# A two-layer graph network on one core: the second layer's step reordered, its results taken after the step's last matrix product

## The chip, the cores and the metric

The kernel runs on one core of a Trainium2 chip. The metric is the device time of one execution in microseconds (us). Before the change the median of 10 runs is 3380.35 us (3376.93 to 3386.58). The engines are TensorE (PE; PEld is its weight load), VectorE (DVE), ScalarE (ACT), GpSimd (POOL) and SyncE (SP), which only issues transfers here.

## What is computed

There are 12500 nodes with 32 features and 200000 edges, sorted by their destination. Two layers follow each other, each as x = x + layer(relu(layernorm(x))). The first sums the scaled source rows of each node's edges and multiplies by a 32x32 matrix. The second puts a small network on every edge and takes the mean over each node's edges:

```python
x_j = x[j_idx]; x_i = x[i_idx]
msg = concatenate([x_i, x_j - x_i], axis=-1)
h = relu(msg @ W1 + b1)      # 64 -> 64
h = relu(h @ W2 + b2)        # 64 -> 128
h = relu(h @ W3 + b3)        # 128 -> 64
m = h @ W4 + b4              # 64 -> 32
s = segment_sum(m, i_idx)
out = s / maximum(cnt, 1)
```

`j_idx` is an edge's source, `i_idx` its destination.

## The kernel before

**What comes before the loop in question.** The first layer (lines 598 to 840) also writes two tables to DRAM, `tab_i` and `tab_j`: for each node its part of `msg @ W1 + b1` as a destination and as a source. What the second layer needs per edge is one row of each, and their sum. The change leaves the first layer alone.

**The second layer** (lines 843 to 999) goes over the edges in chunks of 512 (`CHUNK`: 4 tiles of 128 edges, `TPC`), two chunks at a time. Such a pair takes one step of the loop; there are 391 chunks and so 196 pairs (`NPAIR`). The last pair has one chunk with three tiles of edges. The edges are sorted, so a chunk's destinations lie in a window of 128 nodes, which moves on by 32 nodes (`STEP`) a chunk. For pair m the work is:

- `gather_in` (896): eight indirect transfers that GpSimd issues (line 211), each fetching 128 rows of `tab_j` into `gj`. `gj` has 6 buffers.
- `prepare` (877), three steps ahead: SyncE loads the window of `tab_i` into `ai` (5 buffers) and the edges' relative destinations, spread over all partitions, into `row` (4 buffers).
- `turn` (888): VectorE compares `row` with the partition number (892) and so makes the one-hot matrices that pick rows of `ai`.
- `first` (904): TensorE makes a 1x8 product that only waits for the gathers (908), transposes `gj` (912), and adds the rows of `ai` by the one-hots (916), all into one PSUM tile p1. ScalarE applies relu and writes h1 (920).
- `second` (923): VectorE makes the one-hots of destinations `hot` (584). TensorE multiplies h1 by W2 into p2 (930); ScalarE adds the bias, applies relu and writes h2 (932).
- `third` (934): TensorE multiplies h2 by W3 into p3 (940); VectorE takes the maximum with minus the bias and writes h3 (943).
- `fourth` (947): TensorE sums h3 over the edges of each node with `hot` (958). The sums of two pairs, a group, gather in one half of the PSUM tile `both`, one bank whose halves alternate.
- `add_messages` (962), after each group's second pair: the sums are added to or copied into an accumulator in SBUF by VectorE (560) and ScalarE (558). After four groups `finish_nodes` (853) runs: VectorE prepares counts and the residual (858 to 866), TensorE multiplies by W4 (869), VectorE divides and adds (872, 873) and SyncE writes the rows of `out`.

All of it is under a manual schedule: each engine runs its instructions in the order in which the Python code issues them, and the framework adds the semaphore waits that the data need. The order in a step comes from `lags` and `todo` (977 to 997): at step m the stages `first`, `fourth`, `third`, `second` are issued for different pairs, with the first one step after the gather, the second three, the third four and the fourth five (one less for the last five pairs, but not below one). Each stage issues its matrix products and at once what takes them from PSUM. p1 and p3 have two buffers each, p2 has one.

## Time and profile before

| | |
|---|---|
| median of 10 runs | 3380.35 us |
| the profiled execution, its own time | 3381.98 us |
| its span, from the first to the last instruction | 3380.0 us |
| TensorE busy / VectorE / ScalarE / GpSimd, of the span | 74% / 54% / 33% / 74% |
| the second layer's gathers, first start to last end | 1401.3 to 3352.2 us |
| last VectorE instruction | 3374.65 us |

The profile is one execution. Its page gives each engine's busy time, the costliest groups of instructions (by line and operation, with the idle time of the engine ahead of them and what ended it), and the chain that ended last; the trace answers further questions, such as instructions in order of time, or busy times and the granted TensorE clock of a stretch. A granted clock of 1.00 is full speed. Matrix products are pipelined and their ends modelled, so the distance from one group's start to the next one's is a better price than the stated duration. In float32 each product is shown as several passes, so counts of passes are larger than those of products in the code.

### The profile page before, as it was taken

To read this page: it belongs to the slowest core of one execution; us is meant where nothing else is said; L and a number is where in the kernel's file an instruction comes from. 1 tells how busy PE (TensorE), PEld (TensorE's weight loads), DVE (VectorE), ACT (ScalarE), POOL (GpSimd) and SP (SyncE) were. 2 spreads that over 40 slices of the span, in tenths; PEclk is the share of its full clock that TensorE was granted. 3 is DMA by queue.
4 is the path that set the end of the run, shared out by engine and by line. 5 is a ranking of instruction groups with operands and counts; after the bars stand their busy time and mean duration, and the time that the engine had idled before them with its cause. 6 is when DMAs were issued, how large, how long until landed. Compare 5 with 4: busy or idle time off the path is not lost. (4 is left out here: it accounts for less than half of the span.)

```text
span 3380.0 us, 54122 instructions
## 1 busy us (share of the span) xinstructions
PE 2511.4 (74%) x20860; PEld 1782.5 (53%) x20860; DVE 1815.9 (54%) x4113; ACT 1116.0 (33%) x2034; POOL 2502.0 (74%) x2655
## 2 busy tenths in 40 slices
PE   3772788888888888477778676777777777777777
PEld 2660566666666666244545454545454544545545
DVE  7995787788878887233333333333333333333333
ACT  0003676677666775112122221121212111221121
POOL 7777777777777777477777777777777777777775
PEclk9995998999999998588887888787878788777788
DMA  4113112122222222222222222222222222222221
GB/s 97 15 15 79 26 28 34 31 36 35 32 36 33 33 35 44 44 62 59 62 59 61 62 63 59 61 61 59 62 60 62 59 62 59 63 59 62 60 60 30
DMA packets 234664, 170.64 MB, mean 50 GB/s; under 512 B 156040, under 2 KB 182888, under 8 KB 234400
## 3 DMA queue, kind: packets, MB, share of 16 engines
q0 software_dynamic: 84320, 75.96, 14.1%
q1 hardware_dynamic: 131338, 85.26, 9.4%
q10 hardware_dynamic: 18742, 5.89, 0.9%
q8 instruction: 168, 2.75, 0.3%
q14 instruction: 96, 0.79, 0.1%
HBM read 153.98 MB, written 12.92 MB: 49 GB/s over the span
## 5 line engine op out<-in xcount | busy, mean ns | idle before, releaser
L211 POOL DMA_INDIRECT gj<-tab_j,src_j x1563 | 1474.9, 944 | 511.4 <-issue 420.6
L211 POOL DMA_INDIRECT rows<-tab_hn,src_j x816 | 771.2, 945 | 255.4 <-issue 195.0
L791 ACT ACTIVATE count<-count_two 128x858 bf16<-128x858 f32 x491 | 434.7, 885 | 286.8 <-PE count_two L789 260.1
L943 DVE TENSOR_TENSOR h<-p,b3n 128x512 f32<-128x512 f32 x196 | 135.3, 690 | 727.5 <-PE p L940 727.5
L940 PE MATMUL p<-w3s,h 128*128 128x64 f32 x3128 | 444.7, 302 | 0.0
L940 PEld LDWEIGHTS p<-w3s,h 128*128 128x128 f32 x3128 | 416.9, 215 | 47.1 <-issue 38.7
L932 ACT ACTIVATE h<-p,b2s 128x1024 f32<-128x1024 f32 x196 | 217.8, 1111 | 661.0 <-PE p L930 661.0
L908 PE MATMUL p<-gj,ident 128*1 128x8 f32 x392 | 39.1, 174 | 506.1 <-DMA gj<-tab_j,src_j 506.1
L738 PE MATMUL st<-count,table 128*128 128x104 bf16 (+1 forms) x6076 | 376.3, 217 | 48.0 <-ACT count L791 22.1
L738 PEld LDWEIGHTS <-table 128*128 128x128 bf16 x6076 | 348.8, 99 | 89.8 <-issue 29.4
L908 PEld LDWEIGHTS p<-gj,ident 128*1 128x1 f32 x392 | 21.8, 80 | 678.1 <-issue 666.1
L920 ACT ACTIVATE h<-p 128x512 f32<-128x512 f32 x196 | 117.0, 597 | 790.1 <-PE p L916 790.1
L726 DVE TENSOR_TENSOR oh<-keys,kept 128x2574 bf16<-128x2574 f16 x246 | 365.5, 1488 | 12.3 <-PE count_third L789 12.3
L958 PEld LDWEIGHTS ps<-hot,h 128*64 128x64 f32 x3126 | 270.4, 189 | 174.6 <-issue 164.0
L789 PE MATMUL count_two<-oh,lo 128*128 128x429 bf16 x982 | 276.3, 363 | 93.7 <-ACT count L791 83.8
L560 DVE TENSOR_TENSOR acc<-acc,ps 64x64 f32<-64x64 f32 (+1 forms) x198 | 44.7, 226 | 537.4 <-PE ps L958 504.8
L916 PE MATMUL p<-turned,ai 128*64 128x512 f32 x782 | 328.9, 932 | 0.0
L958 PE MATMUL ps<-hot,h 128*64 128x128 f32 x3126 | 295.6, 351 | 0.5 <-DVE h L943 0.5
L211 POOL DMA_INDIRECT rows_early<-tab_h,src_j x224 | 216.4, 966 | 71.7 <-issue 47.2
L892 DVE TENSOR_TENSOR turned<-row,kept 128x512 f32<-128x512 f16 x391 | 249.7, 680 | 24.5 <-PE p L916 21.4
L791 ACT ACTIVATE count<-count_third 128x416 bf16<-128x416 f32 x491 | 252.0, 513 | 0.0
L584 DVE TENSOR_TENSOR hot<-rel_h,kept 128x512 f32<-128x512 f16 x391 | 249.2, 679 | 0.0
(201 smaller groups left out, 3026.2 us busy)
## 6 DMA issues: line engine op xcount, KB each, us to landing
row<-rel_row SPq DMA_DIRECT2D x195, 256.0 KB
gj<-tab_j,src_j POOLq DMA_INDIRECT x1563
rows<-tab_hn,src_j POOLq DMA_INDIRECT x816
ai<-tab_i SPq DMA_DIRECT2D x195, 64.0 KB
srow<-hi_row SPq DMA_DIRECT2D x64, 98.0 KB
rows_early<-tab_h,src_j POOLq DMA_INDIRECT x224
tab_j<-nu_aij SPq DMA_DIRECT2D x23, 128.0 KB
tab_i<-nu_aij SPq DMA_DIRECT2D x23, 128.0 KB
```

Source lines behind the costliest of these rows:

```text
L211: nc.gpsimd.indirect_dma_start(out=tile_ap, out_offset=None, in_=table, in_offset=bass.IndirectOffsetOnAxis(ap=col, axis=0))
L584: nc.vector.tensor_tensor(hot, rel_h[:, g * TPC : (g + 1) * TPC][:, :, None].to_broadcast([P, TPC, W]), lanes_f[:, None, :W].to_broadcast( ...
L726: nc.vector.tensor_tensor(oh, keys[:, :, i : i + 2][:, :, None, :].to_broadcast([P, 3, KW, 2]), count_h[:, None, :, :].to_broadcast([P, 3, ...
L738: nc.tensor.matmul(ps[:, : tiles * WD], table[:, h, :], c[:, :tiles, h, :], start=(h == 0), stop=(h == PART - 1))
L789: nc.tensor.matmul(ps[:, k, :w], lo[:, i % TPC // 2, :, i % 2], oh[:, k0 + k, :w, i % 2], start=True, stop=True)
L791: nc.scalar.activation(counts[g][:, t, a:b, :].rearrange("p (k h) d -> p k (h d)", k=len(ranges)), ps[:, :, :w], AF.Copy)
L892: nc.vector.tensor_tensor(turned, v["row"][:, k], part_f.to_broadcast([P, CHUNK]), op=OP.is_equal)
L916: nc.tensor.matmul(p1[k * HID : (k + 1) * HID].rearrange("p t e -> p (t e)"), v["ai"][:, k], v["turned"][k], start=False, stop=True, skip_ ...
L932: nc.scalar.activation(h2[:, :n], p2[:, :n], AF.Relu, bias=b2s)
L940: nc.tensor.matmul(p3[:, k * TPC + t, :], v["h2"][:, k, t * P : (t + 1) * P], w3s, start=True, stop=True)
L943: nc.vector.tensor_tensor(h3[:, :n], p3[:, :n], b3n[:, None, :].to_broadcast([P, n, HID]), op=OP.max)
L958: nc.tensor.matmul(ps[k * HID : (k + 1) * HID, o : o + W], v["h3"][:, k * TPC + t, :], v["hot"][k][:, t, :], start=(i == 0 and t == 0), st ...
```

## The change

The lags become fixed: first 1, second 2, third 4, fourth 6 steps after the gather (clipped at the end of the loop, where several pairs then fall in one step). In a step TensorE's work is issued first, in the order `fourth`, `third`, `first`, then a pause's work of `finish_nodes`, then `second`. What takes the products from PSUM is split off into `past_first` to `past_fourth` and issued after all of these, `past_second` first. `ends[step]` is the last product of the step's `second`, and an extra dependency (`behind`) makes h3's instruction wait for it, and the gathers and the loads of `ai` for that of an earlier step. `hot` is made after h3 and no longer ahead of the second stage. The PSUM tiles of the stages are allocated once (`firsts`, `thirds`, `whole`) instead of from pools per pair; `hot` has 3 buffers in place of 4, h1 also. `finish_nodes` has one pause more, ahead of the product with W4. `gather` now returns its instruction.

```diff
     def gather(tile_ap, table, col):
-        nc.gpsimd.indirect_dma_start(
+        return nc.gpsimd.indirect_dma_start(
...
+        firsts = [pp1.tile([P, TPC, P], F32, name=f"p1_{k}") for k in range(2)]
+        thirds = [pp2.tile([P, 2 * TPC, HID], F32, name=f"p3_{k}") for k in range(2)]
+        whole = pp2.tile([P, 2, CHUNK], F32, name="p2")
...
             nc.vector.tensor_add(z, z, x1[:, at, :])
+            yield
             po = message[:, :n]
...
+        ends = {}
+
+        def behind(r, step):
+            if step in ends:
+                tc.add_manual_dep(
+                    r.ins, ends[step].ins.name,
+                    mybir.DependencyInfo(mybir.DependencyClass.Sync, mybir.DependencyReason.DATA))
...
-            nc.sync.dma_start(ai[:, :n], bass.AP(
+            r = nc.sync.dma_start(ai[:, :n], bass.AP(
...
+            behind(r, m - AHEAD - 2)
...
-                gather_chunk(gj[:, :, k, :], tab_j[:, :], g)
+                for t in range(min(TPC, NTR - g * TPC)):
+                    c = g * TPC + t
+                    behind(gather(gj[:, t, k, :], tab_j[:, :], src_j[:, c : c + 1]), m - 5)
...
-            h1 = ep.tile([P, CHUNK], F32, name="h1", bufs=4)
-            nc.scalar.activation(h1, p1.rearrange("p t e -> p (t e)"), AF.Relu)
-            v["h1"] = h1
+            v["p1"] = p1
+
+        def past_first(m):
+            v = live[m]
+            h1 = v["h1"] = ep.tile([P, CHUNK], F32, name="h1", bufs=3)
+            nc.scalar.activation(h1, v["p1"].rearrange("p t e -> p (t e)"), AF.Relu)
 
         def second(m):
...
-                nc.tensor.matmul(p2[:, k], w2s[s, :], v["h1"][s, :], start=True, stop=True)
+                ends[step] = nc.tensor.matmul(p2[:, k], w2s[s, :], v["h1"][s, :], start=True, stop=True)
+
+        def past_second(m):
+            v = live[m]
+            n = len(halves(m))
             h2 = v["h2"] = ep.tile([P, 2, CHUNK], F32, name="h2")
-            nc.scalar.activation(h2[:, :n], p2[:, :n], AF.Relu, bias=b2s)
+            nc.scalar.activation(h2[:, :n], v["p2"][:, :n], AF.Relu, bias=b2s)
...
-            h3 = ep.tile([P, 2 * TPC, HID], F32, name="h3")
-            nc.vector.tensor_tensor(
-                h3[:, :n], p3[:, :n], b3n[:, None, :].to_broadcast([P, n, HID]), op=OP.max)
-            v["h3"] = h3
+
+        def past_third(m):
+            v = live[m]
+            n = len(halves(m)) * TPC
+            h3 = v["h3"] = ep.tile([P, 2 * TPC, HID], F32, name="h3")
+            behind(nc.vector.tensor_tensor(
+                h3[:, :n], v["p3"][:, :n], b3n[:, None, :].to_broadcast([P, n, HID]), op=OP.max), step)
+            v["hot"] = [hot_of(ep, 2 * m + k, f"hot{k}", 3) for k in halves(m)]
...
-        def add_messages(k4):
+        def past_fourth(m):
+            k4, i = divmod(m, GRP // 2)
+            if i < GRP // 2 - 1 and m < NPAIR - 1:
+                return
...
+            for stage, lag in ((first, 1), (second, 2), (third, 4), (fourth, 6)):
+                todo[min(m + lag, NPAIR - 1 + (first, second, third, fourth).index(stage) + 1)].append((m, stage))
+        for step, now in enumerate(todo):
...
+            order = [(m, stage) for stage in (fourth, third, first) for m, s in now if s is stage]
+            for m, stage in order:
+                stage(m)
             advance(running)
...
+            seconds = [m for m, s in now if s is second]
+            for m in seconds:
+                second(m)
+            for m in seconds:
+                past_second(m)
+            for stage in (first, third, fourth):
+                for m, s in order:
+                    if s is stage:
+                        past[stage](m)
+            if step + 1 < NPAIR:
+                turn(step + 1)
```

More of the change, by code (lines that the diff above doesn't have):

```diff
@@ L843, in gnn_kernel @@
     with tc.manual_schedule(), tc.tile_pool(name="prep", bufs=3) as prep, tc.tile_pool(name="e1", bufs=3) as ep, tc.tile_pool(name="fn", bufs=2) as fp, tc.tile_pool(
-        name="p1_ps", bufs=2, space=bass.MemoryType.PSUM
+        name="p1_ps", bufs=1, space=bass.MemoryType.PSUM
     ) as pp1, tc.tile_pool(name="p2_ps", bufs=1, space=bass.MemoryType.PSUM) as pp2:
@@ L901, in gather_in @@
                 g = 2 * m + k
-                gather_chunk(gj[:, :, k, :], tab_j[:, :], g)
+                for t in range(min(TPC, NTR - g * TPC)):
+                    c = g * TPC + t
+                    behind(gather(gj[:, t, k, :], tab_j[:, :], src_j[:, c : c + 1]), m - 5)
         def first(m):
             v = live[m]
-            p1 = pp1.tile([P, TPC, P], F32, name="p1")
+            p1 = firsts[m % 2]
             nc.tensor.matmul(
@@ L918, in first @@
                     start=False, stop=True, skip_group_check=True)
-            h1 = ep.tile([P, CHUNK], F32, name="h1", bufs=4)
-            nc.scalar.activation(h1, p1.rearrange("p t e -> p (t e)"), AF.Relu)
-            v["h1"] = h1
+            v["p1"] = p1
[3 more added lines that the diff above has]
+            nc.scalar.activation(h1, v["p1"].rearrange("p t e -> p (t e)"), AF.Relu)
         def second(m):
             v = live[m]
-            v["hot"] = [hot_of(ep, 2 * m + k, f"hot{k}", 4) for k in halves(m)]
-            n = len(halves(m))
-            p2 = pp2.tile([P, 2, CHUNK], F32, name="p2")
+            p2 = v["p2"] = whole
             for k in halves(m):
                 s = slice(k * HID, (k + 1) * HID)
-                nc.tensor.matmul(p2[:, k], w2s[s, :], v["h1"][s, :], start=True, stop=True)
+                ends[step] = nc.tensor.matmul(p2[:, k], w2s[s, :], v["h1"][s, :], start=True, stop=True)
+        def past_second(m):
+            v = live[m]
+            n = len(halves(m))
             h2 = v["h2"] = ep.tile([P, 2, CHUNK], F32, name="h2")
-            nc.scalar.activation(h2[:, :n], p2[:, :n], AF.Relu, bias=b2s)
+            nc.scalar.activation(h2[:, :n], v["p2"][:, :n], AF.Relu, bias=b2s)
         def third(m):
             v = live[m]
-            n = len(halves(m)) * TPC
-            p3 = pp2.tile([P, 2 * TPC, HID], F32, name="p3", bufs=2)
+            p3 = v["p3"] = thirds[m % 2]
             for k in halves(m):
@@ L975, in gnn_kernel @@
         turn(0)
-        def lags(m):
-            less = min(1, max(0, m - (NPAIR - 6)))
-            return [max(1, lag - less) for lag in (1, 3, 4, 5)]
-        stages = (first, second, third, fourth)
+        past = {first: past_first, second: past_second, third: past_third, fourth: past_fourth}
         todo = [[] for _ in range(NPAIR + 6)]
         for m in range(NPAIR):
-            for stage, lag in zip(stages, lags(m)):
-                todo[m + lag].append((m, stage))
-        for m, now in enumerate(todo):
-            if m < NPAIR:
-                gather_in(m)
-            if m + AHEAD + 1 < NPAIR:
-                prepare(m + AHEAD + 1)
-            advance(running)
-            for k, stage in now:
-                stage(k)
-                if stage is fourth and (k % (GRP // 2) == GRP // 2 - 1 or k == NPAIR - 1):
-                    add_messages(k // (GRP // 2))
-            if m + 1 < NPAIR:
-                turn(m + 1)
+            for stage, lag in ((first, 1), (second, 2), (third, 4), (fourth, 6)):
+                todo[min(m + lag, NPAIR - 1 + (first, second, third, fourth).index(stage) + 1)].append((m, stage))
+        for step, now in enumerate(todo):
+            if step < NPAIR:
+                gather_in(step)
+            if step + AHEAD + 1 < NPAIR:
+                prepare(step + AHEAD + 1)
+            order = [(m, stage) for stage in (fourth, third, first) for m, s in now if s is stage]
+            for m, stage in order:
+                stage(m)
+            advance(running)
+            seconds = [m for m, s in now if s is second]
[9 more added lines that the diff above has]
+                turn(step + 1)
         while running:
```

## The prediction

> **What bounds the kernel now.** I read the page's costliest groups first, for the second layer's loop (the lines from 908 on). Columns: busy, mean ns of one | idle before, what ended it.

> ```profile
> L211 POOL DMA_INDIRECT gj<-tab_j,src_j x1563 | 1474.9, 944 | 511.4 <-issue 420.6
> L908 PE MATMUL p<-gj,ident 128*1 128x8 f32 x392 | 39.1, 174 | 506.1 <-DMA gj<-tab_j,src_j 506.1
> ```

> The gathers fill GpSimd. Of the 511.4 us idle, 35.35 stands ahead of the very first gather (timeline, 1401.29 us: it waits for the first layer's last table rows). The rest is (1474.9 + 511.4 - 35.35)/1563 = 1.248 us a gather, 0.944 of work and 0.30 of issue, with no longer gap. A step has eight: 9.98 us. TensorE's first matmul of a step, L908, waits for a gather to land. So GpSimd sets 1401 to 3352 us, and TensorE follows.

> Next the busy time by stretches: the loop, then three stretches around its end. Columns: length, busy time (instructions) of PE, PEld, DVE, ACT, POOL, granted TensorE clock, DMA share, GB/s.

> ```profile
> 1401.00:3350.00 1949.00, 1445.29 (x9060) 952.08 (x9060) 676.52 (x1330) 384.51 (x618) 1472.98 (x1561) 0.80 0.27 60
> 3340.00:3351.00 11.00, 9.04 (x70) 6.60 (x72) 4.32 (x13) 2.12 (x4) 8.48 (x9) 0.84 0.14 28
> 3351.00:3365.00 14.00, 14.00 (x63) 9.21 (x65) 2.38 (x5) 1.90 (x3) 0.94 (x1) 0.52 0.06 11
> 3365.00:3380.00 15.00, 7.76 (x67) 6.06 (x64) 4.48 (x14) 1.09 (x2) 0.00 (x0) 0.84 0.04 9
> ```

> In the loop TensorE works 1445/195 = 7.41 us a step and has about 2.5 spare. After the last gather (3352.2) GpSimd is idle and TensorE with its followers sets the end: the **drain**, from 3350.17, when pair 194's first stage starts, to 3374.65, when the last VectorE instruction ends.

> Last the timeline, for the price of each stage. First a step at full clock, then rows of the drain:

> ```profile
> 1502.53 0.20 PE L908 MATMUL p<-gj,ident 128*1 128x8 f32 x2 [1.78 <-DMA gj<-tab_j,src_j]
> 1502.66 0.65 PE L912 MATMUL p<-ident,gj 128*128 128x128 f32 x4
> 1503.24 1.08 PE L916 MATMUL p<-turned,ai 128*64 128x512 f32 x4
> 1504.15 1.04 PE L958 MATMUL ps<-hot,h 128*64 128x128 f32 x16
> 1505.13 2.00 PE L940 MATMUL p<-w3s,h 128*128 128x64 f32 x16
> 1507.05 1.13 PE L930 MATMUL p<-h,w2s 64*128 64x512 f32 x4
> ...
> 3354.10 1.98 PE L958 MATMUL ps<-hot,h 128*64 128x128 f32 x16
> 3356.01 3.68 PE L940 MATMUL p<-w3s,h 128*128 128x64 f32 x16
> 3359.61 2.08 PE L930 MATMUL p<-h,w2s 64*128 64x512 f32 x4
> ...
> 3371.44 0.87 PE L958 MATMUL ps<-hot,h 128*64 128x128 f32 x6 [0.52 <-DVE h L943]
> ```

> From start to start, at full clock: first stage 1.62, fourth 0.98, third 1.92, second 1.13, together 5.65. At half clock: fourth 1.85 (1495.54 to 1497.39), third 3.60, second 2.08, first 2.94 (1492.60 to 1495.54), together 10.47.

> **The change part by part.** Call E the end of a step's second stage, now TensorE's last work in every step that has one.

> *Gathers, index loads.* Count and order on GpSimd and SyncE stay the same, and the first gather keeps its waits. Gather m now waits for E of step m-5 in place of the first stage in that step: four steps, 40 us, old. The ai load waits for E of the step before and is needed three to four steps later; the row load queued behind it on SyncE is needed two steps later, some 20 us. All of it costs nothing under that cover. Without cover, each late us of TensorE would be one of the whole loop.

> *A new wait on TensorE.* VectorE's and ScalarE's work on a step's products now starts after E: 0.11 us (the observed gap from L930's end to L932), then L943 0.61 and two L584 1.19 start to start, then the accumulator: add, copy, add, copy (L560, L558), 2515.60 to 2516.68, 1.08. The next fourth stage starts a step with the matmuls into the one bank that these copies read, so every second step, after a group's end, TensorE waits 0.11 + 0.61 + 1.19 + 1.08 + 0.06 = **3.05 us**. Before, the sums were taken in the middle of a step, under the third stage. Queued behind it are that step's third, first and second stages, and on them ScalarE's and VectorE's next round. Per two steps TensorE needs 2 x 7.41 + 3.05 = 17.9 us, GpSimd 19.97. GpSimd hides it, with 2.1 us to spare. So **the loop gains and loses nothing**: TensorE's idle 2.5 us is not the bound, and no instruction leaves GpSimd.

> *Lags.* The fourth stage runs 6 steps after the gather and not 5, the third 4, so more work is left when the gathers end. Full clock, from 3350.17:
> - Step 195, first and second: 1.62 + 1.13. E = 3352.92.
> - Step 196: wait 3.05, fourth 0.98, third 1.92, half a first (last pair, one chunk: 0.13 + 0.58 + 0.46), second 1.13. E = 3361.17.
> - Step 197: fourth 0.98, third 1.92, half a second 0.56. E = 3364.63.
> - Step 198: the wait, with the longer sums of a node group's end (3345.49 to 3347.32, 1.83 instead of 1.08): 3.80; fourth 0.98, third 1.92: 3371.33. Half a third follows under VectorE's work.
> - Step 199: the last fourth needs VectorE's L943 and two L584 of pair 194, then L943 and L584 of pair 195: 0.11 + 0.61 + 1.19 + 0.42 + 0.68, and 0.04 to start: 3374.38, and 0.87: 3375.25.
> - VectorE: four sums 1.39 (two took 0.67 at 3372.35), one result 0.60, five small operations 1.05, the other result 0.55: end 3378.84.

> That is **4.2 us** later than 3374.65. All at half clock (the same sum with 2.94, 1.85, 3.60, 2.08, the waits unchanged) it ends near 3393.4: **18.75 us** later. Which clock? The stretch 3351 to 3365 shows TensorE without a pause and still 0.52 granted, so in a drain with two waits of 3 to 4 us and a third in step 199 about half of the work should run at half clock, as in before's own drain: (4.2 + 18.75)/2 = **11.5 us**.

> [...]

> *Fixed PSUM tiles, smaller hot and h1 rings, one more pause in the node finish.* Two p1, two p3 and one p2 tile were there before; the readers of a step end about 3 us after E, and the same tile is written again later than that. Nothing either way in the loop (cover: GpSimd's 2.1 us); in the drain they are in the sum.

> **Sum.** 3381.98 for the profiled execution (span 3380.0 and 2.0 around it) + 0 in the loop + 11.5 in the drain = 3393.5. It lies 1.6 above the median of the runs shown, 3380.35, so on the median's scale 3391.9; I say **3392 us**, 0.34% slower. A measurement of this kernel can tell about 0.2%, 6.8 us.

> **Rivals.**
> 1. *Not slower: the drain runs at nearly full clock.* Place: steps 195 to 199. Price +4.2 us, 3384.5. It decides while less than (6.8 - 4.2)/(18.75 - 4.2) = 18% of the drain's work is at half clock. For it: 0.84 granted on both sides of the slow stretch. Against it: 0.52 within, and the waits that the change adds there. 13%.
> 2. *TensorE becomes the bound.* The 3.05 us wait itself lowers the clock, and third and fourth now come first after it. Two steps then cost 3.05 + 11.3 + 9.64 x the share of work at half clock; past 58% this exceeds 19.97. At 65% it is 20.6, 0.33 us a step, over 195 steps +64: 3456 with the drain. At 100% 24.0, +395. For it: single steps of 10 to 12 us (1841.95: 11.98). Against it: 0.80 granted over the loop, and that TensorE, when late, has no idle time left to lower it. 8%.
> 3. *Faster.* The drain alone can't do it: at full clock and with the waits of steps 196 and 198 gone it is 4.2 - 3.05 - 3.80 = -2.65 us, within 0.2%. It would take cheaper gathers: 0.01 us off the 0.30 of issue is 1563 x 0.01 = 16 us, 3376 with the drain. Nothing on GpSimd changes, so 3%.
> 4. *The waits don't do what they say*, being met at once by other work: then only the lags are left, -2.65 at full clock and some +5 with half of the work slow: 3378 to 3385. 4%.

> **How the numbers follow.** The forecast, a late drain with an unchanged loop, has 72%, 3387 to 3399. Rival 2 is slower too: 8%. Rivals 1 and 4 lie within 0.2%: 17%. Rival 3: 3%. So slower 0.80, same 0.17, faster 0.03. The range, 3381 to 3408, leaves out rival 2's far part, rival 3 and a little of rival 4; its upper part holds the half-clock drain, 3380.35 + 18.75 = 3399, and a TensorE just past its limit (0.05 us a step).

> **What would show it.** In the changed kernel's profile: the gather group still 1.248 us each, the last starting near 3351.3; a wait of L984 on ScalarE's L558, some 3 us, about 95 times; from the last gather's landing to VectorE's end about 36 us where it was 24.5. It is wrong if gathers show gaps that end on PE (rival 2), if L984 doesn't wait, or if the end comes as early as before.

## The result, and the profile after

The changed kernel takes **3393.64 us** (median of 8 runs, 3390.16 to 3394.79) against 3380.85 (28 runs of the kernel before on the same chip): ratio **1.0037**, 95% interval 1.0028 to 1.0045. That is 12.8 us slower.

One correction to what stands ahead of the prediction. In the code of before a step begins with its oldest pair: fourth, third, second, first. The order given there is the same cycle, begun at the wait. So before already went oldest first, and what the change moves on TensorE is the first stage, from behind the second to ahead of it.

The costliest groups of the changed kernel, that answer to those shown of before (busy, mean ns of one | idle time before, what ended it):

```profile
L211 POOL DMA_INDIRECT gj<-tab_j,src_j x1563 | 1475.0, 944 | 511.5 <-issue 448.7
L984 PE MATMUL ps<-hot,h 128*64 128x128 f32 x3126 | 277.5, 334 | 288.1 <-ACT acc L558 275.8
```

The gathers are where they were: the same 944 ns, 511.5 us of idle time against 511.4. What is new is the second line, 288 us of idle time. Before, the same products were L958 and had 0.5:

```profile
L958 PE MATMUL ps<-hot,h 128*64 128x128 f32 x3126 | 295.6, 351 | 0.5 <-DVE h L943 0.5
```

The waits of the changed kernel in the loop, 1401 to 3350 us, show where it was taken from (us in total, times, longest):

```profile
PE ps L984 <- ACT acc L558: 272.9, 91, 3.1
PE p L926 <- DMA gj<-tab_j,src_j: 116.5, 64, 16.0
```

Before, TensorE waited in the loop almost for the gathers alone, at L908 (L926 now):

```profile
PE p L908 <- DMA gj<-tab_j,src_j: 504.3, 177, 16.0
```

273 us of that are now a wait for the sums, 3.0 us each time, and most of the rest went into a slower clock. The loop and the drain by stretches (length, busy time of PE, PEld, DVE, ACT, POOL, granted clock, DMA share, GB/s):

```profile
1401.00:3350.00 1949.00, 1557.71 (x9022) 994.14 (x9022) 666.49 (x1310) 361.46 (x614) 1471.46 (x1560) 0.75 0.27 60
...
3351.02:3384.94 33.92, 27.02 (x170) 21.56 (x170) 12.95 (x37) 3.58 (x8) 0.00 (x1) 0.70 0.03 5
```

In the loop the clock fell from 0.80 to 0.75, and TensorE's work rose from 1445 to 1558 us. It cost nothing, since GpSimd sets the pace. The second line is the drain, from the end of the last gather to the end of VectorE's last instruction: 33.92 us, where before had 22.43 (3352.22 to 3374.65). The timeline of TensorE shows what it is made of:

```profile
3346.80 0.20 PE L926 MATMUL p<-gj,ident 128*1 128x8 f32 x2
...
3348.52 1.13 PE L949 MATMUL p<-h,w2s 64*128 64x512 f32 x4
3352.62 1.09 PE L984 MATMUL ps<-hot,h 128*64 128x128 f32 x16 [2.97 <-ACT acc L558]
3353.65 3.20 PE L962 MATMUL p<-w3s,h 128*128 128x64 f32 x16
...
3364.42 1.12 PE L949 MATMUL p<-h,w2s 64*128 64x512 f32 x2
3369.26 1.98 PE L984 MATMUL ps<-hot,h 128*64 128x128 f32 x16 [3.71 <-DVE acc L560]
3371.16 5.38 PE L962 MATMUL p<-w3s,h 128*128 128x64 f32 x24
3376.47 4.96 PE L984 MATMUL ps<-hot,h 128*64 128x128 f32 x38
```

The two waits for the sums, 2.97 and 3.71 us, are no longer hidden by gathers. Around the end of each the clock falls to half for a while: it is 0.50 from 3354.20 to 3361.03 and from 3367.85 to 3381.51 us (16 passes of L962 take 3.20 us, where 2.00 is full clock; 24 take 5.38, where 2.89 is). At the end three fourth stages stand in a row.

One execution's first layer may end some us earlier or later than another's (the first gather starts at 1401.29 us before, at 1397.84 in the changed kernel), so the traces are best compared from the first gather on. In the loop column of this table stands the time from the first gather's start to the last one's end, in the drain column the time from there to the end of VectorE's last instruction, and beside it the clock granted in the drain. The kernels are explained below; "us against before" is the difference of loop plus drain.

| kernel | ratio of medians (95%) | loop | drain | clock in the drain | us against before |
|---|---|---|---|---|---|
| before | 1 | 1950.9 | 22.4 | 0.71 | 0 |
| changed | 1.0037 (1.0028 to 1.0045) | 1953.2 | 33.9 | 0.70 | +13.7 |
| changed, sums early | 1.0012 (1.0003 to 1.0021) | 1951.4 | 25.8 | 0.89 | +3.9 |
| changed, spare products | 1.0016 (1.0007 to 1.0025) | 1952.1 | 26.7 | 0.98 | +5.4 |
| changed, last pairs forward | 1.0069 (1.0056 to 1.0082) | 1955.5 | 39.3 | 0.61 | +21.4 |
| changed, sums early, last pairs forward | 1.0032 (1.0021 to 1.0044) | 1955.3 | 29.5 | 0.70 | +11.5 |
| before, longer lags | 1.0017 (1.0008 to 1.0026) | 1950.8 | 26.7 | 0.68 | +4.2 |
| before, spare products | 0.9989 (0.9980 to 0.9998) | 1950.7 | 16.6 | 1.00 | -6.1 |
| before, short lags | 0.9982 (0.9973 to 0.9992) | 1952.4 | 15.1 | 0.95 | -5.8 |
| before, short lags and spare products | 0.9995 (0.9986 to 1.0004) | 1952.3 | 16.0 | 0.98 | -5.1 |

### The profile page after: what moved, and what is told of

The parts are those of the page before. It is cut to its first block, busy times and chain, and to the rows that moved or that the text cites. A ratio compares the mean times of both kernels' runs of the same rounds, so it can differ in the third digit from the quotient of the medians.

```text
span 3390.2 us, 54031 instructions
## 1 busy us (share of the span) xinstructions
PE 2629.4 (78%) x20860; PEld 1830.9 (54%) x20860; DVE 1813.4 (53%) x4113; ACT 1094.4 (32%) x2034; POOL 2502.0 (74%) x2655
## 4 chain that ended last, share of the span: by engine, by line
POOL 34%; issue 14%; DMA 7%; PE 5%; DVE 2%; ACT 0%; SPq 0%; POOLq 0%; ACTq 0%; DVEq 0%
POOL gj L211 34%; DMA gj<-tab_j,src_j 6%; PE p L962 1%; PE p L949 1%; PE p L934 1%; PE ps L984 1%; PE p L930 0%; DVE hot L584 0%; PE nu_ps L512 0%; PE nu_ps L473 0%; PE st L738 0%; DVE acc L560 0%; DVE h L969 0%; DVE oh L726 0%; DMA rows<-tab_hn,src_j 0%
## 5 line engine op out<-in xcount | busy, mean ns | idle before, releaser
L211 POOL DMA_INDIRECT gj<-tab_j,src_j x1563 | 1475.0, 944 | 511.5 <-issue 448.7
L211 POOL DMA_INDIRECT rows<-tab_hn,src_j x816 | 770.7, 945 | 254.0 <-issue 193.5
L962 PE MATMUL p<-w3s,h 128*128 128x64 f32 x3128 | 545.6, 347 | 0.0
L962 PEld LDWEIGHTS p<-w3s,h 128*128 128x128 f32 x3128 | 514.0, 257 | 46.9 <-issue 46.9
L984 PE MATMUL ps<-hot,h 128*64 128x128 f32 x3126 | 277.5, 334 | 288.1 <-ACT acc L558 275.8
L984 PEld LDWEIGHTS ps<-hot,h 128*64 128x64 f32 x3126 | 218.3, 168 | 484.3 <-ACT acc L558 361.1
L934 PE MATMUL p<-turned,ai 128*64 128x512 f32 x782 | 308.0, 876 | 0.0
L949 PE MATMUL p<-h,w2s 64*128 64x512 f32 x782 | 284.0, 809 | 0.0
L211 POOL DMA_INDIRECT rows_early<-tab_h,src_j x224 | 216.6, 967 | 71.8 <-issue 48.8
L908 DVE TENSOR_TENSOR turned<-row,kept 128x512 f32<-128x512 f16 x391 | 250.4, 682 | 28.6 <-PE p L934 22.6
L584 DVE TENSOR_TENSOR hot<-rel_h,kept 128x512 f32<-128x512 f16 x391 | 249.3, 679 | 0.0
L789 PEld LDWEIGHTS <-lo 128*128 128x128 bf16 x1473 | 131.5, 100 | 178.5 <-issue 119.3
L949 PEld LDWEIGHTS p<-h,w2s 64*128 64x128 f32 x782 | 78.5, 246 | 225.4 <-issue 224.3
L342 PE MATMUL deg_ps<-hi,lo 128*128 128x98 bf16 x1563 | 159.3, 271 | 44.4 <-DVE lo L325 44.4
```

What stands on the lines that cost most here:

```text
L211: return nc.gpsimd.indirect_dma_start(out=tile_ap, out_offset=None, in_=table, in_offset=bass.IndirectOffsetOnAxis(ap=col, axis=0))
L584: nc.vector.tensor_tensor(hot, rel_h[:, g * TPC : (g + 1) * TPC][:, :, None].to_broadcast([P, TPC, W]), lanes_f[:, None, :W].to_broadcast( ...
L789: nc.tensor.matmul(ps[:, k, :w], lo[:, i % TPC // 2, :, i % 2], oh[:, k0 + k, :w, i % 2], start=True, stop=True)
L908: nc.vector.tensor_tensor(turned, v["row"][:, k], part_f.to_broadcast([P, CHUNK]), op=OP.is_equal)
L934: nc.tensor.matmul(p1[k * HID : (k + 1) * HID].rearrange("p t e -> p (t e)"), v["ai"][:, k], v["turned"][k], start=False, stop=True, skip_ ...
L949: ends[step] = nc.tensor.matmul(p2[:, k], w2s[s, :], v["h1"][s, :], start=True, stop=True)
```

## The experiments

**The sums at once.** Theory: what the drain lost is mostly the wait for the sums. Rival: it is the lags.

```diff
             for m, stage in order:
                 stage(m)
+                if stage is fourth:
+                    past_fourth(m)
...
-            for stage in (first, third, fourth):
+            for stage in (first, third):
```

> The changed kernel with one part undone: a group's sums (past_fourth) are issued right after the fourth stage's products again, so they run under the third stage; order, lags and all other late readers stay. My theory, that all of the loss sits in the drain after the last gather and that the loop hides TensorE's wait: the waits of L984 on L558 go (3.05 us every second step), the gathers stay at 1.248 us each, and only the drain gains, 3.05 + 3.80 us of waits and 1 to 3 us of clock: 3384 to 3388, against 3393.6 of the changed kernel. Rival, that the waits in the loop cost time as well: more than 12 us below the changed kernel, at or under the kernel before. Rival, that only the longer lags cost: no gain, 3392 to 3395.

Measured: 3383.9 us (11 runs), ratio 1.0012 (1.0003 to 1.0021), at the lower end of what the theory expected. TensorE's idle time is back at the gathers, as the page shows:

```profile
L926 PE MATMUL p<-gj,ident 128*1 128x8 f32 x392 | 39.1, 175 | 509.8 <-DMA gj<-tab_j,src_j 509.7
```

So of the 12.8 us some 8.5 (1.0037 - 1.0012, times 3380) go with taking the sums late. Not all of that is waiting: the drain's clock rose too, from 0.70 to 0.89. The rest stays with lags, order and the other late readers.

**Longer lags alone.** The kernel before, its order and its readers unchanged, with the lags of the change:

```diff
-        def lags(m):
...
-            for stage, lag in zip(stages, lags(m)):
-                todo[m + lag].append((m, stage))
+            for i, (stage, lag) in enumerate(zip(stages, (1, 2, 4, 6))):
+                todo[min(m + lag, NPAIR + i)].append((m, stage))
```

> The kernel before with only the change's lags, 1, 2, 4 and 6, clipped at the end as in the change, once more for the same reason; order and readers as before. Theory (longer lags leave one third stage and two fourth stages more behind the last gather): 1.92 + 2 x 0.98 = 3.9 us at full clock, 3.60 + 2 x 1.85 = 7.3 at half; ratio to before 1.0010 to 1.0023. Rival (the lags cost nothing, all of the loss is the late sums and the clock they bring): 0.9994 to 1.0006.

Measured: 3385.55 us (11 runs), before beside it 3378.25; ratio 1.0017 (1.0008 to 1.0026), in the middle of what was expected. Loop as before, drain 26.7 against 22.4 us. Together with the run above this splits the loss as it was measured, each part with the clock that came with it: the lags are worth 4 to 6 us, the late sums 8 to 10, which is a little more than the 12.8 to be shared out. A split at one clock follows below.

**The clock in the drain of the changed kernel.** Four spare products in each of the two waits of the drain keep TensorE streaming and take nothing away:

```diff
+            if step in (NPAIR, NPAIR + 2):
+                v = live[NPAIR - 1]
+                for _ in range(4):
+                    nc.tensor.matmul(
+                        firsts[1][:HID].rearrange("p t e -> p (t e)"), v["ai"][:, 0], v["turned"][0], start=True, stop=True)
             for m, stage in order:
                 stage(m)
```

> The changed kernel with spare products in the waits of steps 196 and 198, once more, for the same reason. Theory (the clock that these waits bring makes most of the drain's loss): 5 to 9 us faster than the changed kernel, ratio to before 1.0012 to 1.0024. Rival (the readers behind E set the end, the clock is worth little): 1.0032 to 1.0044.

Measured: 3386.99 us (11 runs), ratio 1.0016 (1.0007 to 1.0025), as the theory expected; in the traces the drain is 7.2 us shorter than that of the changed kernel. The timeline around the second wait (L1021 are the spare products):

```profile
3365.01 3.65 PE L1021 MATMUL p<-turned,ai 128*64 128x512 f32 x8
3368.79 1.09 PE L984 MATMUL ps<-hot,h 128*64 128x128 f32 x16
3369.82 2.89 PE L962 MATMUL p<-w3s,h 128*128 128x64 f32 x24
3372.64 2.95 PE L984 MATMUL ps<-hot,h 128*64 128x128 f32 x38
```

The fourth stage starts as late as without them, 4.83 us behind the start of the second (4.84 without), for it still waits for the sums. What comes behind runs at full clock, 0.98 over the drain: 24 passes of L962 in 2.89 us and not 5.38, 38 of L984 in 2.95 and not 4.96.

**The clock in the drain of before.** The same question on the other side: three spare products ahead of L908, in TensorE's wait for the gathers, for pairs 191 to 194.

```diff
             p1 = pp1.tile([P, TPC, P], F32, name="p1")
+            if NPAIR - 5 <= m < NPAIR - 1:
+                for _ in range(3):
+                    nc.tensor.matmul(
+                        p1[:HID].rearrange("p t e -> p (t e)"), v["ai"][:, 0], v["turned"][0], start=True, stop=True)
```

> The same kernel as the one with spare products before L908 for pairs 191 to 194, once more, since before itself took 4304 us in that call, with TensorE short of instructions. Theory (before's own drain is slow because the clock stays at half from 3351.3 to 3364.9): 4 to 6.5 us faster than before, ratio 0.9981 to 0.9989. Rival (the drain is set by GpSimd's last gathers and by the readers): 0.9997 to 1.0003, or 1.0005 to 1.0010 by the spare products' own time.

Measured: 3375.92 us (11 runs), before beside it 3380.78; ratio 0.9989 (0.9980 to 0.9998), as the theory expected. The drain of before, and that of this kernel, by the same columns as above:

```profile
3352.22:3374.65 22.43, 20.54 (x124) 15.19 (x122) 6.86 (x19) 2.99 (x4) 0.00 (x0) 0.71 0.03 6
```

```profile
3346.56:3363.12 16.56, 14.67 (x124) 11.04 (x122) 6.87 (x19) 3.00 (x4) 0.01 (x1) 1.00 0.05 8
```

The same 124 passes of TensorE, the same VectorE and ScalarE work: 14.67 us of TensorE instead of 20.54. Half clock was 5.9 us of before's own drain. This matters for the account: at full clock on both sides, changed against before is loop plus drain 1978.8 against 1967.3, and 3386.99 against 3375.92 us in the medians, taken side by side. **The change costs 11 us at an equal clock.** Half clock costs either drain 6 to 8 us and adds only some 2 us to the difference.

One more trace splits these 11 us at full clock. A second execution of before with the longer lags (from the set of runs described further down, where the loop was slower) had a drain at 1.00. From the start of pair 194's first stage to the end of VectorE's last instruction, by the same columns: before with spare products, before with the longer lags, the changed kernel with spare products.

```profile
3344.94:3363.12 18.18, 16.29 (x133) 11.74 (x132) 6.87 (x19) 3.00 (x4) 1.32 (x2) 1.00 0.06 11
4288.76:4311.19 22.43, 19.89 (x182) 15.35 (x180) 10.78 (x32) 4.52 (x7) 0.67 (x1) 1.00 0.04 8
3349.07:3379.10 30.03, 28.35 (x200) 17.81 (x200) 14.28 (x39) 4.84 (x9) 2.69 (x3) 0.98 0.04 8
```

The longer lags alone cost 4.25 us, the order and the late readers 7.6 more (11.9 together from this start), of which the two waits for the sums are 6.7 (2.97 and 3.71 in the changed kernel).

**Fewer steps behind the last gather, two misses.** In the changed kernel the last pairs were pulled forward: third lag 3 and fourth lag 4 for the last five, fourth lag 5 for the three ahead of them.

```diff
-            for stage, lag in ((first, 1), (second, 2), (third, 4), (fourth, 6)):
+            late = m - (NPAIR - 8)
+            for stage, lag in ((first, 1), (second, 2), (third, 3 if late >= 3 else 4), (fourth, 4 if late >= 3 else 5 if late >= 0 else 6)):
```

> The changed kernel with the lags of the last eight pairs shortened in the last steps with gathers (third 3 and fourth 4 for the last five pairs, fourth 5 for the three ahead), so that two fourth stages and one third stage fewer are left for the drain, as in the kernel before. Late sums and order stay. Theory: the drain loses 2 x 0.98 + 1.92 = 3.9 us of products at full clock, 7.3 at half: 3386 to 3391. Rival, that only the late waits cost: 3392 to 3395.

Measured: 3402.16 us (6 runs), ratio 1.0069 (1.0056 to 1.0082): slower than the changed kernel, against the expectation. Its timeline:

```profile
3349.71 3.63 PE L984 MATMUL ps<-hot,h 128*64 128x128 f32 x32 [4.76 <-ACT acc L558]
...
3361.78 1.97 PE L984 MATMUL ps<-hot,h 128*64 128x128 f32 x16 [3.72 <-DVE acc L560]
...
3372.85 0.43 PE L984 MATMUL ps<-hot,h 128*64 128x128 f32 x2 [1.39 <-DVE hot L584]
```

The expectation took it that TensorE has time left in the last steps for the work that is pulled forward. It hasn't: the first stage of pair 194 starts 1955.9 us after the first gather, in the changed kernel 1949.0. And where a fourth stage comes only one step behind its third, it waits for the one-hots (L584) too, which this order makes only after the second stage. With the sums at once added to these lags the same was expected to be as fast as before, within 0.1%:

> Both at once: sums issued right after the fourth stage and the shorter lags at the end, the rest of the change (order, fixed tiles, late readers of the other stages, late dependencies of gathers and loads) kept. Theory: the two parts of the drain add up to the whole loss, so 3379 to 3384, the kernel before within 0.1%. Rival, that something else of the change costs too (a cost in the loop, or the late readers themselves): 3386 or more.

Measured: 3390.68 us (6 runs), ratio 1.0032 (1.0021 to 1.0044), a miss as well. The waits for the sums are gone, those for the one-hots stand in nearly every step of the drain:

```profile
3344.39 2.13 PE L984 MATMUL ps<-hot,h 128*64 128x128 f32 x18 [1.48 <-DVE hot L584]
...
3353.96 1.59 PE L984 MATMUL ps<-hot,h 128*64 128x128 f32 x16 [1.48 <-DVE hot L584]
```

So long lags and late readers belong together: with the readers behind the last product, a shorter lag is paid for in waits.

**Short lags, early readers.** The kernel before with lags 1, 1, 2 and 3 in every step, in the order first, fourth, third, second:

```diff
-            less = min(1, max(0, m - (NPAIR - 6)))
-            return [max(1, lag - less) for lag in (1, 3, 4, 5)]
+            return [1, 1, 2, 3]
...
+        ranks = {first: 0, fourth: 1, third: 2, second: 3}
...
-            for k, stage in now:
+            for k, stage in sorted(now, key=lambda each: ranks[each[1]]):
```

> The kernel before with lags 1, 1, 2, 3 for all pairs and the order first, fourth, third, second in a step, so that a pair's second stage runs in the step of its first, behind the fourth and third of older pairs: one step less is left after the last gather. If the drain alone decides, with GpSimd the bound of the loop: one step less, some 5.6 us at full clock and more at half, 3369 to 3376. If the shorter lags make TensorE wait for h2 or h3 in the loop beyond its spare 2.5 us a step, slower: 3400 and more. If the drain's end is set by something else, no change, 3378 to 3383.

Measured: 3373.82 us (10 runs), ratio 0.9982 (0.9973 to 0.9992): **faster than both kernels**. The size was expected, but the reason lies elsewhere than in the lags. Before shortens the lags of its last five pairs already, and behind the first stage of pair 194 both have the same stages, but for one product with W4 that comes earlier here. From that start to VectorE's end it takes 18.65 us (3350.36 to 3369.01), before 24.48. Of the 5.8 us, 1.85 are the price of that product in before's drain (L869, 3352.25 to 3354.10); the other 4 us go with the clock, 0.95 in the drain where before has 0.71:

```profile
3353.92:3369.01 15.09, 13.21 (x104) 9.56 (x100) 6.86 (x19) 2.40 (x3) 0.01 (x1) 0.95 0.05 9
```

If so, it and the spare products win the same thing, and both together hardly more:

> The kernel before with lags 1, 1, 2 and 3 in every step and the three spare products ahead of L908 for pairs 191 to 194, once more for the same reason. Theory (clock: 3.4 us of the drain with the short lags alone are at half clock and hold some 1.7 us too much): 1 to 2 us faster than the short lags alone, ratio to before 0.9976 to 0.9980. Rival (nothing left to gain): 0.9982, or up to 0.9990 if the spare products delay the last pair.

Measured: 3376.32 us (11 runs), ratio 0.9995 (0.9986 to 1.0004): not the 1 to 2 us more that the theory wanted. In its trace the drain is at 0.98, but the spare products of the last step hold up the first stage of pair 194, which starts at 3352.34 us and not at 3350.36, and that takes back what the clock gives. Whether it is truly slower than the short lags alone is open: the intervals overlap.

**The same kernels with gaps in TensorE's work.** Four of these kernels also ran in a set, the only one on its chip, in which everything took over a quarter longer, before itself 4303.98 us (11 runs). What was expected of them:

> The changed kernel with four spare products of 128x64 by 128x512, whose result nothing reads, put into TensorE's two long waits of the drain: ahead of the fourth stage in steps 196 and 198 (2.97 and 3.71 us of wait in the changed kernel's trace, ending at 3352.62 and 3369.26). Theory (the clock that these waits bring makes most of the drain's loss): the stretches 3354 to 3361 and 3368 to 3382 run at full clock, which takes 3.4 and some 5 us off TensorE's 19 us in them; 5 to 9 us faster than the changed kernel, ratio to before 1.0012 to 1.0024. Rival (the readers behind E set the end, the clock is worth little): no more than 2 us faster or slower than the changed kernel, 1.0032 to 1.0044.

> The kernel before with only the change's lags, 1, 2, 4 and 6, clipped at the end as in the change; order and readers as before. Theory (longer lags leave one third stage and two fourth stages more behind the last gather): 1.92 + 2 x 0.98 = 3.9 us at full clock, 3.60 + 2 x 1.85 = 7.3 at half; ratio to before 1.0010 to 1.0023. Rival (the lags cost nothing, all of the loss is the late readers and the clock they bring): 0.9994 to 1.0006.

> The kernel before with three spare products of 128x64 by 128x512, whose result the first stage overwrites, put ahead of L908 in the steps of pairs 191 to 194, into TensorE's wait for the gathers. They take nothing away; they only give TensorE more columns to stream just before the drain. Theory (before's own drain is slow because the clock stays at half from 3351.3 to 3364.9): at full clock the stages in that stretch take 6 us less; 4 to 6.5 us faster than before, ratio 0.9981 to 0.9989. Rival (the drain is set by GpSimd's last gathers and by the readers, not by the clock): within 1 us, 0.9997 to 1.0003, or slower by the spare products' own 1.6 to 3.3 us, 1.0005 to 1.0010.

> The kernel before with lags 1, 1, 2 and 3 in every step and, in addition, the three spare products ahead of L908 for pairs 191 to 194. In the trace of the short lags alone 3.4 us of the drain (3351.3 to 3354.7) are at half clock and hold some 1.7 us too much. Theory (clock): 1 to 2 us faster than the short lags alone, ratio to before 0.9976 to 0.9980. Rival (nothing left to gain): 0.9982, or up to 0.9990 if the spare products delay the last pair.

Measured: 1.0302 (1.0278 to 1.0325) for the changed kernel with spare products, 1.0033 (1.0012 to 1.0053) for before with the longer lags, 1.0036 (1.0015 to 1.0057) for before with spare products and 1.0144 (1.0119 to 1.0169) for the short lags with them. These ratios tell little of the drain, for which the other runs of the same kernels stand above, but something of a rival in the prediction. One group of the longer lags in this set:

```profile
L940 PE MATMUL p<-w3s,h 128*128 128x64 f32 x3128 | 506.2, 312 | 152.6 <-issue 152.1
```

The same kernel in the other set:

```profile
L940 PE MATMUL p<-w3s,h 128*128 128x64 f32 x3128 | 450.2, 305 | 0.0
```

152 us of gaps inside a group that elsewhere runs without one, with no releaser that the profile shows. That TensorE's instructions came late, as one expectation above has it, would fit but is not shown: the page's larger instruction queue (q8) has the same 168 packets in both, at 0.3% of the span here and 0.4% there. The cause is open. With such gaps TensorE is late in places where GpSimd was the bound, and then the change's wait is not hidden. The waits of the changed kernel with spare products over the whole of this execution:

```profile
PE ps L984 <- ACT acc L558: 492.8, 83, 7.9
...
POOL gj L211 <- PE p L949: 436.8, 97, 7.2
```

From first to last gather it took 2456 us, before with longer lags 2339, with spare products 2331: some 120 us, 0.6 us a step, for a kernel whose loop costs nothing more while GpSimd is the bound. How much of that is the wait is not shown: the short lags with spare products, which have no such wait, took 2394 here.

## Why the prediction was right, point by point

- **GpSimd sets the loop; the loop gains and loses nothing.** Right. From the first gather's start to the start of pair 194's first stage: 1948.88 us before, 1948.96 after.
- **A new wait of 3.05 us every second step, hidden with 2.1 us to spare.** Right: 3.0 us, 91 times in the loop. The spare time was less. The clock in the loop fell to 0.75, TensorE needs 1557.7/195 = 7.99 us a step, two steps with a wait 18.95 of 19.97, so 1.0 us was left. The runs with gaps show what may lie beyond it.
- **Gathers and index loads at no cost.** Right for the time, but one queue was overlooked: the last pair's buffer is cleared by VectorE (L915), which now stands behind E of step 194. The last three gathers start 2.15 us late (2.45 of idle time ahead of them instead of 0.30). TensorE came later than they did, so the end didn't move.
- **The drain at full clock, 28.67 us from pair 194's first stage.** The changed kernel with spare products, at 0.98, took 3379.10 - 3349.07 = 30.03. The 1.4 us are mostly two terms that were mis-sized: "half a first (last pair, one chunk: 0.13 + 0.58 + 0.46)" and "half a second 0.56". One chunk's products take as long as two (see the last section), 1.0 for 0.46 and 1.05 for 0.56.
- **Step 199 waits for VectorE.** It didn't. With the products at half clock, VectorE's work was done in time, and the last fourth stages ran without a pause (4.96 us). The sum came out alike, as half-clock products took the place of the wait.
- **About half of the drain's work at half clock, +11.5 us.** The drain took 3384.94 - 3346.80 = 38.14 us from the same start, 13.7 more than before. That lies 65% of the way from the full-clock sum to the half-clock sum, not 50%. On the median: +12.8 measured, +11.7 forecast. The half was taken over from before's drain and not worked out, so that the number came this close is partly luck.
- **What the difference is made of.** Here the prediction's account was misleading, though its number was not. It measured the changed drain at full clock, "+4.2 us", against before's own drain with all its half clock, so that nearly two thirds of the loss seemed to be the clock's. At an equal clock the difference is 11 us: 4.25 for the longer lags, and most of the rest for the two uncovered waits, 2.97 + 3.71. The clock takes nearly as much from both (6 and 8 us).
- **The rivals.** 1, nearly full clock: it didn't come by itself, but with spare products it is 1.0016, +5.4 us, where +4.2 was worked out. 2, TensorE the bound: not in these runs, though 1 us from it in two steps (the clock in the loop is lower with the waits, 0.75, where the changed kernel with the sums at once has 0.81), and in places in the set with gaps, whose cause is open. 3, cheaper gathers: 944 ns each, as before. 4, waits met at once: no, 91 of 3.0 us.

In before's drain a busy TensorE did not bring the clock back: from 3351.48 to 3365.13 us it was busy without a pause (13.65 of 13.65 us), at 0.50 throughout. In the changed kernel's drain half clock came with the wait of 2.97 us, 1.6 us behind its end, as well as with that of 3.71.

## What to carry to other kernels

Work that is hidden in a loop has to be priced again at the loop's end: there nothing covers a wait, and every step of lag is a step more behind the last transfer. When results are taken late, what the next step overwrites first should not be taken last; here taking the sums straight behind their products won back two thirds of the loss (8.5 of 12.8 us). Compare two versions at the same granted clock before giving the clock a share of the difference.

## What the runs showed of the hardware

**One chunk's products cost as much as two.** In the timeline of before, for pair 195 with one chunk and at full clock:

```profile
3367.74 1.12 PE L930 MATMUL p<-h,w2s 64*128 64x512 f32 x2
```

Two passes in 1.12 us, where the four of a pair with two chunks take 1.13. In the trace those four start two by two (1507.056 and 1507.063 us, 1507.590 and 1507.596), the two of one chunk one after the other (3367.743 and 3368.277). In the code the two chunks' operands lie on different partitions, 0 to 63 and 64 to 127. So half the work saved nothing here.
